# Cross-attention on one core: a reordered and partly rewritten tail for the last four of 64 batches

## The chip, the core and the metric

The kernel runs on one core of a Trainium2 chip. A core has five engines that work beside each other: TensorE (matmuls, PE in the profile, with its weight loads as PEld), VectorE (DVE), ScalarE (ACT), GpSimd (POOL) and SyncE (SP), which here issues all DMAs. Each engine executes its own instructions in the order in which they were written; between engines, semaphores order the work. The metric is device time in microseconds (us), the median of three runs.

## The reference

For each of 64 batches there is a text `x` (256 rows of 512) and a context `c` (256 rows of 384). All is float32.

```python
text_p  = x @ W_text + b_text                      # 256 x 512
audio_p = c @ W_audio + b_audio                    # 256 x 512
Q = layer_norm(text_p, g1, beta1)
K = layer_norm(audio_p, g2, beta2)
alpha = softmax(Q @ K.T / sqrt(512))               # 256 x 256
H = (alpha @ audio_p) @ W_out + b_out
out = layer_norm(H + x, g_out, beta_out)           # 256 x 512
```

Since the rows of `alpha` sum to one, the kernel multiplies `alpha` with `c` itself and folds `W_audio @ W_out` into one weight `wao` and both biases into one row `bao`.

## The kernel before

A batch has two row tiles of 128 rows (`LT = ST = 2`), on 128 partitions. For a batch the kernel computes, in this order:

- the projections q and k, each as seven products of half size (class `Blocks`, `products` on TensorE, L442, `leave` on VectorE, L453, which adds each product into the rows where it belongs). Products 3, 5, 6 and 7 use sums of the input blocks that GpSimd makes beforehand;
- their normalisation on ScalarE and GpSimd. `rstd_of` (L306) is two small GpSimd instructions: L310 or L312 adds the epsilon, L314 raises to the power -0.5;
- a round trip through DRAM in 32 x 32 squares (`store`, `fetch`), and a transpose of the squares on VectorE (`turn`, L91), to get qT and kT; `affine` (L416, ScalarE) applies gamma and beta in four chunks;
- the scores (L481), their row maxima (L491, VectorE), the exponentials with their row sums (L498, ScalarE) and the reciprocals of the sums (L508);
- eT, the transposed exponentials: in the loop by a trip through DRAM, and in the last two batches by TensorE (`transpose_e`, L530) with a copy by ScalarE (`copy_e`, L536);
- the context `ps_z = c.T @ eT` (`context`, L547) and its copy zT (L554, ScalarE);
- the output. In all batches but the last two it is made by the seven products: `start_products` (L556) makes the sums `zsum` (L290 to L293, GpSimd), then `last.o.products` and `last.o.leave`, and `add_x` (L563, GpSimd) adds the input. In the last two batches `multiply(t)` (L593, three matmuls of 512 columns for row tile t) and `evict(t)` (L602, VectorE, which divides by the row sum and adds `x + bao`) do it, and `add_bias` (L655, GpSimd) has made `x + bao` before;
- the last layer norm. For the seven-product batches `statistics` (L565) has ScalarE pass over each row tile twice (L571 for the mean, L576 for the squares); for the last two batches `moments` (L238, L239) takes mean and variance on VectorE. Then VectorE runs `shift` (L618 or L622: minus mean, times gamma) and `settle` (L627: times rstd, plus beta) on each tile; `finish` is both for both tiles;
- `store` (L637), a DMA of the batch's rows.

The order is written out by hand: `tc.manual_schedule()` keeps the instructions of each engine in the order of the program. The loop handles several batches at once (`done` is two batches behind `at`, `last` one behind). It ends with batch 61; the lines from L858 on handle the last four: `done` is batch 60, `last` 61, `at` 62 and `end` 63. The queues that matter there before the change:

- GpSimd: `add_x` of `done`; `add_bias` of 62; rstd of `done`; the four `zsum` of `last`; `add_x` of `last`; `add_bias` of 63; rstd of `last`; rstd of `at`; rstd of each tile of `end`.
- ScalarE: exponentials of `at`; zT of `last`; four passes of statistics of `done`; affine of qT; eT of `at`; affine of kT; zT of `at`; four passes of statistics of `last`; exponentials of `end`.
- SyncE: after the loads of batch 63 only the stores of 60, 61, 62 and of the two tiles of 63.

Buffers are shared in rotation. The output rows (tag `yr`) have two: the tile of `at` reuses that of `done` and waits for its store, and the tile of `end` that of `last`. PSUM has six banks for products, outputs and transposes (`p_pj`) and two for scores and context (`p_at`).

Of the kernel before, what the change touches and what calls it, by code (L numbers as in the profile page):

```python
# [9 lines left out]
F32 = mybir.dt.float32  # L10
AF = mybir.ActivationFunctionType
ALU = mybir.AluOpType
# [3 lines left out]
P = 128  # L16
# [6 lines left out]
def kernel(  # L23
# [41 lines left out]
    nc = tc.nc  # L65
    ctx.enter_context(tc.manual_schedule())
    B, L, D = x.shape
    S, DA = c.shape[1:]
    H = w_text.shape[1]
    LT, ST = L // P, S // P  # L70
    DC, AC, HC = D // P, DA // P, H // P
# [7 lines left out]
    small = ctx.enter_context(tc.tile_pool(name="small", bufs=4))  # L79
    scratch = ctx.enter_context(tc.tile_pool(name="scratch", bufs=3, space=bass.MemoryType.DRAM))  # L80
    p_pj = ctx.enter_context(tc.tile_pool(name="p_pj", bufs=6, space=PSUM))
# [43 lines left out]
    def row(v, name):  # L125
        t = const.tile([P, H], F32, tag=name, name=name)
        nc.sync.dma_start(t, v.rearrange("(o h) -> o h", o=1).broadcast_to([P, H]))
        return t
# [23 lines left out]
    def take_columns():  # L152

        ps = p_at.tile([P, P], F32, tag="at", name="ps_v")
        nc.tensor.transpose(ps, vectors, ident)
        nc.scalar.copy(columns, ps[:, : 5 * HC].rearrange("p (n k) -> p n k", n=5))
        return [columns[:, n, :] for n in range(5)]
# [51 lines left out]
    wao_sb = const.tile([P, AC, D], F32, tag="wao", name="wao")  # L209
# [25 lines left out]
    def moments(mv, src, t):  # L235

        st = small.tile([P, 6], F32, tag="st", name="st")
        nc.vector.bn_stats(st, src)  # L238
        nc.vector.bn_aggr(mv[:, t, :], st)  # L239
# [15 lines left out]
    H2 = H // 2  # L255
# [50 lines left out]
    def rstd_of(var, n, total=False):  # L306

        ve = small.tile([P, n], F32, tag="ve", name="ve")
        if total:
            nc.gpsimd.tensor_scalar(ve, var, 1.0 / D, EPS, ALU.mult, ALU.add)  # L310
        else:
            nc.gpsimd.tensor_scalar(ve, var, EPS, None, ALU.add)  # L312
        r = small.tile([P, n], F32, tag="rstd", name="rstd")
        nc.gpsimd.tensor_tensor(r, ve, nhalf[:, :n], ALU.pow)  # L314
        return [r[:, t : t + 1] for t in range(n)]

    class Projection:
# [40 lines left out]
        def scales(self):  # L358
            if self.centred:
                self.r = rstd_of(self.var, self.nt)  # L360
                return
            self.r = rstd_of(self.mv[:, :, 1], self.nt)
            self.nmr = small.tile([P, self.nt], F32, tag="nmr", name="nmr")
            for t in range(self.nt):
                nc.gpsimd.tensor_scalar(
                    self.nmr[:, t : t + 1],
                    self.mv[:, t, 0:1],
                    self.r[t],
                    -1.0,
                    ALU.mult,  # L370
                    ALU.mult,
                )
# [96 lines left out]
    class Attention:  # L469
# [140 lines left out]
            moments(self.mv, self.y[:, t, :], t)  # L610

        def scales(self, lo=0, n=LT):
            self.r = {lo + t: r for t, r in enumerate(rstd_of(self.mv[:, lo : lo + n, 1], n))}

        def shift(self, t):
            row = self.y[:, t, :]
            if hasattr(self, "o"):
                nc.vector.scalar_tensor_tensor(  # L618
                    row, row, self.nm[:, t : t + 1], go_sb, ALU.add, ALU.mult
                )  # L620
            else:
                nc.vector.scalar_tensor_tensor(  # L622
                    row, row, self.mv[:, t, 0:1], go_sb, ALU.subtract, ALU.mult
                )
# [27 lines left out]
    def add_bias(b):  # L652
        xb = rows[b][0]
        for t in range(LT):
            nc.gpsimd.tensor_tensor(xb[:, t, :], xb[:, t, :], bao_sb, ALU.add)  # L655

    assert B > 3
    q, k, xT, cT, rows = {}, {}, {}, {}, {0: (x_0, c_0)}
# [61 lines left out]
    g1_sb, be1_sb, g2_sb, be2_sb, bac_sb = take_columns()  # L720
# [45 lines left out]
    beo_sb = row(beta_out, "beo")  # L766

    done = last = None
    for b in range(B - 2):
        three = b + 3 < B  # L770
        at = Attention(b)
# [83 lines left out]
        done, last = last, at  # L855


    at = Attention(B - 2)  # L858
# [8 lines left out]
    last.turn_e()  # L867
    at.maxima()
    at.exponentials()
    add_bias(B - 2)  # L870
    last.context()
    done.statistics()
    at.reciprocals()
    q[B - 1].turn()
    last.start_products()
    q[B - 1].affine(g1_sb, be1_sb)
    at.transpose_e()
    at.copy_e()
    last.o.products(1, 2)
    last.o.leave(1)  # L880
    last.o.products(6, 5)
    k[B - 1].turn()
    last.o.leave(6)
    last.o.leave(2)
    last.o.leave(5)
    last.o.products(7, 3)
    last.o.leave(3)
    last.o.leave(7)
    last.o.products(4)
    last.o.leave(4)  # L890
    last.add_x()
    k[B - 1].affine(g2_sb, be2_sb)
    add_bias(B - 1)
    at.context()
    done.finish()
    done.store()
    end = Attention(B - 1)
    end.scores(end=True)
    at.start_output()
    at.multiply(0)  # L900
    last.statistics()
    end.maxima()
    end.exponentials()
    end.reciprocals()
    at.evict(0)
    at.multiply(1)
    end.transpose_e()
    end.copy_e()
    last.finish()
    last.store()  # L910
    at.evict(1)
    at.scales()
    end.context()
    at.finish()
    at.store()
    end.start_output()
    for t in range(LT):
        end.multiply(t)
        end.evict(t)
        end.scales(t, 1)  # L920
        end.finish(t, 1)
        end.store(t, 1)


# [30 lines left out]
```

## Time and profile before

| what | value |
|---|---|
| time, median of 3 runs | 1429.02 us (1428.93 to 1429.34) |
| the profiled execution, its time | 1430.98 us |
| its span in the profile | 1429.2 us |
| busy over the span: PE, DVE, ACT, POOL | 98%, 89%, 66%, 61% |
| scores of batch 62 end | 1384.4 us |
| scores of batch 63 end | 1405.3 us |
| last matmul ends | 1419.67 us |
| last VectorE instruction ends | 1426.16 us |

In the profile a line such as `L627 DVE` is an instruction of that line of the kernel before on that engine. Times in the chain and the timeline are microseconds from the start of the span. The chain is followed back from the last instruction: at each step to what released it, or to the instruction before it on its engine. A TensorE matmul in float32 is recorded as two instructions, so 128 x 256 columns twice is one matmul of the program.

### The profile page before, as it was taken

How to read it: one execution, taken by the hardware profiler on the slowest of the kernel's cores; microseconds unless marked ns; L12 is line 12 of the kernel's file. 1: busy time of each engine (PE TensorE's matmuls, PEld its weight loads, DVE VectorE, ACT ScalarE, POOL GpSimd, SP SyncE). 2: the span in 40 equal slices, each digit the busy share in tenths (PEclk: the TensorE clock that was granted, in tenths of full speed). 3: DMA queues.
4: the chain of work that ended last, by engine and by line, in shares of the span. 5: the costliest groups of instructions: out<-in, count | busy, mean ns of one | idle time of the engine just before them, and what ended most of it. 6: DMA issues, size and time to landing. Idle time of an engine off the chain costs nothing.

```text
span 1429.2 us, 23268 instructions
## 1 busy us (share of the span) xinstructions
PE 1406.8 (98%) x6419; PEld 1219.1 (85%) x6419; DVE 1270.3 (89%) x2123; ACT 937.5 (66%) x2309; POOL 874.7 (61%) x1293
## 2 busy tenths in 40 slices
PE   7999999999999999999999999999999999999997
PEld 4788888888888888888888888888888888888874
DVE  5789999999999999999999999999999999999976
ACT  4576676676676676676676766766766766766762
POOL 4556666666666666666666566576566566666643
PEclk9999999999999999999999999999999999999998
DMA  9798787887887788788788788888878888877761
GB/s 206 215 250 232 232 239 221 234 242 218 238 234 229 231 230 235 231 231 235 227 224 243 232 223 242 236 221 240 240 223 232 246 219 232 242 221 231 222 191 60
DMA packets 450294, 322.61 MB, mean 226 GB/s; under 512 B 154740, under 2 KB 382580, under 8 KB 450164
## 3 DMA queue, kind: packets, MB, share of 16 engines
q1 hardware_dynamic: 450164, 321.11, 79.8%
q8 instruction: 53, 0.87, 0.3%
q14 instruction: 77, 0.63, 0.2%
HBM read 204.09 MB, written 116.92 MB: 225 GB/s over the span
## 4 chain that ended last, share of the span: by engine, by line
PE 96%; DVE 1%; DMA 1%; POOL 0%; ACT 0%; SPq 0%; issue 0%; POOLq 0%; DVEq 0%
PE ps_q L442 27%; PE ps_k L442 21%; PE ps_y L442 21%; PE ps_sc L481 15%; PE ps_z L547 11%; DMA wt<-in_L_xattn_W_text_dram 1%; PE ps_wao L216 1%; PE ps_q L332 0%; DVE yr L627 0%; DVE yr L618 0%; DVE y L602 0%; DVE st L238 0%; DMA out_dram<-yr 0%; DVE y L627 0%; POOL ve L312 0%
## 5 line engine op out<-in xcount | busy, mean ns | idle before, releaser
L481 PE MATMUL ps_sc<-kT,qT 128*128 128x256 f32 x1024 | 231.7, 379 | 0.0
L312 POOL TENSOR_SCALAR ve<-var 128x2 f32<-128x2 f32 x126 | 44.9, 356 | 304.1 <-ACT junk L350 304.1
L498 ACT ACTIVATE e<-ps_sc,nmx 128x256 f32<-128x256 f32 x128 | 59.5, 469 | 247.5 <-DVE nmx L491 247.5
L453 DVE TENSOR_TENSOR qr<-ps_q,qr 128x512 f32<-128x512 f32 x378 | 188.2, 511 | 35.8 <-PE ps_q L442 23.8
L481 PEld LDWEIGHTS ps_sc<-kT,qT 128*128 128x128 f32 x1024 | 194.2, 190 | 27.6 <-ACT kT L416 0.9
L453 DVE TENSOR_TENSOR kr<-ps_k,kr 128x512 f32<-128x512 f32 x378 | 188.1, 511 | 24.3 <-PE ps_k L442 0.5
L453 DVE TENSOR_TENSOR yr<-ps_y,yr 128x512 f32<-128x512 f32 x372 | 185.1, 511 | 27.5 <-PE ps_y L442 3.8
L563 POOL TENSOR_TENSOR yr<-yr,x 128x512 f32<-128x512 f32 x124 | 156.9, 1275 | 62.9 <-DVE yr L453 62.9
L547 PE MATMUL ps_z<-eT,c 128*128 128x256 f32 x768 | 176.6, 379 | 0.8 <-ACT eT L536 0.7
L442 PE MATMUL ps_q<-wtsum,xsum 128*128 128x256 f32 x756 | 173.4, 379 | 0.0
L314 POOL TENSOR_TENSOR rstd<-ve,nhalf 128x2 f32<-128x2 f32 (+1 forms) x193 | 158.6, 822 | 16.1
L442 PE MATMUL ps_k<-wa,cT 128*128 128x256 f32 x630 | 166.8, 379 | 0.0
L442 PE MATMUL ps_y<-wao,zT 128*128 128x256 f32 x620 | 164.7, 380 | 0.0
L547 PEld LDWEIGHTS ps_z<-eT,c 128*128 128x128 f32 x768 | 145.8, 190 | 21.2 <-ACT eT L536 0.9
L442 PEld LDWEIGHTS ps_q<-wtsum,xsum 128*128 128x128 f32 x756 | 143.6, 190 | 19.5
L350 ACT ACTIVATE junk<-kr 128x512 f32<-128x512 f32 x126 | 79.4, 630 | 98.0 <-DVE kr L453 98.0
L442 PEld LDWEIGHTS ps_k<-wa,cT 128*128 128x128 f32 x630 | 119.6, 190 | 16.2
L416 ACT ACTIVATE qT<-qT,columns 128x256 f32<-128x256 f32 x256 | 133.0, 592 | 0.4 <-DVE qT L91 0.4
L378 ACT ACTIVATE kr<-kr,rstd 128x512 f32<-128x512 f32 x126 | 84.0, 714 | 74.8 <-POOL rstd L314 74.8
L416 ACT ACTIVATE kT<-kT,columns 128x256 f32<-128x256 f32 x256 | 132.3, 590 | 0.4 <-DVE kT L91 0.3
L442 PEld LDWEIGHTS ps_y<-wao,zT 128*128 128x128 f32 x620 | 118.2, 191 | 16.2
L627 DVE SCALAR_TENSOR_TENSOR yr<-yr,rstd,beo 128x512 f32<-128x512 f32 x124 | 128.3, 1071 | 0.3
(140 smaller groups left out, 2944.8 us busy)
## 6 DMA issues: line engine op xcount, KB each, us to landing
x<-in_x_dram SPq DMA_DIRECT2D x64, 512.0 KB, 4.3
kd<-kr SPq DMA_DIRECT2D x64, 512.0 KB, 3.1
kq<-kd SPq DMA_DIRECT2D x256, 128.0 KB, 3.4
qd<-qr SPq DMA_DIRECT2D x64, 512.0 KB, 5.1
qq<-qd SPq DMA_DIRECT2D x256, 128.0 KB, 3.3
xq<-in_x_dram SPq DMA_DIRECT2D x252, 128.0 KB, 2.8
out_dram<-yr SPq DMA_DIRECT2D x62, 512.0 KB, 4.8
cq<-in_ctx_dram SPq DMA_DIRECT2D x252, 96.0 KB, 2.5
```

Of the source, the lines that this page charges most:

```text
L312: nc.gpsimd.tensor_scalar(ve, var, EPS, None, ALU.add)
L314: nc.gpsimd.tensor_tensor(r, ve, nhalf[:, :n], ALU.pow)
L350: nc.scalar.activation(junk, self.rows[:, t, :], AF.Square, scale=1.0 / math.sqrt(H), accum_out=self.var[:, t : t + 1],)
L378: nc.scalar.mul(row, row, self.r[t])
L416: nc.scalar.activation(self.T[:, k, :], self.T[:, k, :], AF.Identity, bias=bet[:, k : k + 1], scale=gam[:, k : k + 1],)
L442: nc.tensor.matmul(bank[:, j, :], lhsT=side, rhs=w, start=(i == 0), stop=(i == len(pairs) - 1))
L453: add = lambda o, i0, i1: nc.vector.tensor_tensor(o, i0, i1, ALU.add)
L481: nc.tensor.matmul(self.sc[:, t, :], lhsT=self.qT[:, k, bass.ts(t, P)], rhs=self.kT[:, k, :], start=(k == 0), stop=(k == HC - 1),)
L498: nc.scalar.activation(self.e[:, t, :], self.sc[:, t, :], AF.Exp, bias=self.nmx[:, t : t + 1], accum_out=self.den[:, t : t + 1],)
L547: nc.tensor.matmul(ps[:, j, :], lhsT=self.c_sb[:, s, bass.ts(lo + j, P)], rhs=self.eT[:, s, :], start=(s == 0), stop=(s == ST - 1),)
L563: nc.gpsimd.tensor_tensor(self.y[:, t, :], self.y[:, t, :], self.xb[:, t, :], ALU.add)
L627: nc.vector.scalar_tensor_tensor(self.y[:, t, :], self.y[:, t, :], self.r[t], beo_sb, ALU.mult, ALU.add)
```

## The change

Nothing in the loop changes but a test of an attribute (`shift` picks its mean from `nm`, which `statistics` sets, or else from `mv`). In the tail:

- `done` and `last` take their statistics by `moments` on VectorE instead of `statistics` on ScalarE. The new method also issues their rstd at once. For `done` this comes ahead of `reciprocals` of `at` and, on GpSimd, ahead of `add_bias(B - 2)`; for `last` it comes behind `exponentials` of `end`.
- `done.finish()` is taken apart: both shifts stand ahead of `start_products`, both settles where `finish` stood.
- Product 4 of `last` is multiplied as the third, ahead of 6 and 5. The transposes of q and k (`turn`) and their `affine` move: q behind the first products, k behind `leave(2)`.
- `end.transpose_e` and `end.copy_e` come between `at.multiply(0)` and `at.multiply(1)`.
- The start and the first product of `end`'s output stand ahead of `at.finish()`.
- The second tile of `end` is multiplied, evicted, settled and stored in two halves of 256 columns; its statistics are two `bn_stats` joined by one `bn_aggr`. The work on the two tiles of `end` is interleaved.

```diff
         def scales(self, lo=0, n=LT):
-            self.r = {lo + t: r for t, r in enumerate(rstd_of(self.mv[:, lo : lo + n, 1], n))}
+            self.r = getattr(self, "r", {})
+            self.r.update({lo + t: r for t, r in enumerate(rstd_of(self.mv[:, lo : lo + n, 1], n))})
+
+        def moments(self):
+            self.mv = small.tile([P, LT, 2], F32, tag="mvy", name="mvy")
+            for t in range(LT):
+                moments(self.mv, self.y[:, t, :], t)
+            self.scales()
+
+        def multiply_halves(self, t):
+            self.ps_h = []
+            for h in range(2):
+                ps = p_pj.tile([P, H2], F32, tag="pj", name="ps_y")
+                self.ps_h.append(ps)
+                for k in range(AC):
+                    nc.tensor.matmul(
+                        ps,
+                        lhsT=self.zT[:, k, bass.ts(t, P)],
+                        rhs=wao_sb[:, k, bass.ts(h, H2)],
+                        start=(k == 0),
+                        stop=(k == AC - 1),
+                    )
+
+        def evict_halves(self, t):
+            st = small.tile([P, 2, 6], F32, tag="st2", name="st2")
+            for h in range(2):
+                half = self.y[:, t, bass.ts(h, H2)]
+                nc.vector.scalar_tensor_tensor(
+                    half,
+                    self.ps_h[h],
+                    self.rden[:, t : t + 1],
+                    self.xb[:, t, bass.ts(h, H2)],
+                    ALU.mult,
+                    ALU.add,
+                )
+                nc.vector.bn_stats(st[:, h, :], half)
+            nc.vector.bn_aggr(self.mv[:, t, :], st)
+
+        def settle_halves(self, t):
+            for h in range(2):
+                half = self.y[:, t, bass.ts(h, H2)]
+                nc.vector.scalar_tensor_tensor(
+                    half, half, self.r[t], beo_sb[:, bass.ts(h, H2)], ALU.mult, ALU.add
+                )
+                nc.sync.dma_start(out[self.b, bass.ts(t, P), bass.ts(h, H2)], half)
...
     at.exponentials()
+    done.moments()
+    at.reciprocals()
     add_bias(B - 2)
     last.context()
-    done.statistics()
-    at.reciprocals()
-    q[B - 1].turn()
+    done.shift(0)
+    done.shift(1)
     last.start_products()
-    q[B - 1].affine(g1_sb, be1_sb)
     at.transpose_e()
     at.copy_e()
     last.o.products(1, 2)
+    q[B - 1].turn()
     last.o.leave(1)
+    last.o.products(4)
+    q[B - 1].affine(g1_sb, be1_sb)
     last.o.products(6, 5)
-    k[B - 1].turn()
     last.o.leave(6)
     last.o.leave(2)
+    k[B - 1].turn()
+    k[B - 1].affine(g2_sb, be2_sb)
     last.o.leave(5)
     last.o.products(7, 3)
     last.o.leave(3)
     last.o.leave(7)
-    last.o.products(4)
     last.o.leave(4)
     last.add_x()
-    k[B - 1].affine(g2_sb, be2_sb)
     add_bias(B - 1)
     at.context()
-    done.finish()
+    done.settle(0)
+    done.settle(1)
     done.store()
     end = Attention(B - 1)
     end.scores(end=True)
     at.start_output()
     at.multiply(0)
-    last.statistics()
     end.maxima()
     end.exponentials()
+    last.moments()
     end.reciprocals()
     at.evict(0)
-    at.multiply(1)
     end.transpose_e()
     end.copy_e()
+    at.multiply(1)
     last.finish()
     last.store()
     at.evict(1)
     at.scales()
     end.context()
+    end.start_output()
+    end.multiply(0)
     at.finish()
     at.store()
-    end.start_output()
-    for t in range(LT):
-        end.multiply(t)
-        end.evict(t)
-        end.scales(t, 1)
-        end.finish(t, 1)
-        end.store(t, 1)
+    end.evict(0)
+    end.scales(0, 1)
+    end.multiply_halves(1)
+    end.shift(0)
+    end.evict_halves(1)
+    end.scales(1, 1)
+    end.settle(0)
+    end.store(0, 1)
+    end.shift(1)
+    end.settle_halves(1)
```

More of the change, by code (lines that the diff above doesn't have):

```diff
@@ L612, in scales @@
         def scales(self, lo=0, n=LT):
-            self.r = {lo + t: r for t, r in enumerate(rstd_of(self.mv[:, lo : lo + n, 1], n))}
+            self.r = getattr(self, "r", {})
[39 more added lines that the diff above has]
+                nc.sync.dma_start(out[self.b, bass.ts(t, P), bass.ts(h, H2)], half)
         def shift(self, t):
             row = self.y[:, t, :]
-            if hasattr(self, "o"):
+            if hasattr(self, "nm"):
                 nc.vector.scalar_tensor_tensor(
```

## The prediction

> **What bounds the kernel now.** I read the page first, then the chain of waits and the timeline of the last 50 us, then the windows there. The page says that TensorE is the bound for the whole (busy 98% of the span, 96% of the chain). The change leaves everything up to the scores of batch 62 as it was, so only what follows 1384.4 us of the 1429.2 us span can move. Batches 60, 61, 62, 63 are `done`, `last`, `at`, `end` there. The chain in order of time, where it leaves TensorE:
>
> ```profile
> 1387.82 1.23 ACT junk L571 x4
> 1389.05 1.42 ACT junk L576 x4
> 1390.46 0.08 issue
> 1390.54 0.20 POOL ve L310
> 1390.74 0.07 issue
> 1390.82 0.70 POOL rstd L314
> 1391.52 0.43 POOL zsum L290
> 1391.94 0.07 issue
> 1392.01 0.47 POOL zsum L291
> 1392.48 0.04 issue
> 1392.52 6.77 PE ps_y L442 x16
> ```
>
> ScalarE's statistics of `done` hold the rstd in POOL's queue, and `zsum` stands behind it, so TensorE has nothing from 1389.14 to 1392.52, 3.38 us. The windows over that stretch show what follows; the columns are length, busy time and count of the five engines, the granted TensorE clock, DMA share and GB/s:
>
> ```profile
> 1389.00:1392.50 3.50, 0.14 (x1) 0.00 (x0) 1.79 (x3) 3.50 (x10) 1.80 (x5) 0.91 0.84 271
> 1392.50:1395.00 2.50, 2.48 (x6) 2.03 (x7) 0.69 (x1) 2.16 (x5) 1.07 (x2) 0.50 0.03 11
> ```
>
> The clock falls to half. Windows of half a microsecond put the fall at 1391.87 and the return at 1398.69, 6.82 us later, twice 3.41. So 16 matmul records took 6.77 us where 16 at full clock take 16 x 0.2155 = 3.45 (0.2155 is the start-to-start distance of 128x256 records in the scores).
>
> The timeline shows two more costs, POOL beside VectorE, and a store:
>
> ```profile
> 1384.39 2.49 POOL L655 TENSOR_TENSOR x<-x,bao 128x512 f32<-128x512 f32 x2
> ...
> 1400.50 1.57 DVE L627 SCALAR_TENSOR_TENSOR yr<-yr,rstd,beo 128x512 f32<-128x512 f32 x1
> ...
> 1401.49 3.41 POOL L655 TENSOR_TENSOR x<-x,bao 128x512 f32<-128x512 f32 x2
> ...
> 1408.34 0.75 DVE L602 SCALAR_TENSOR_TENSOR y<-ps_y,rden,x 128x512 f32<-128x512 f32 x1 [1.04 <-DMA out_dram<-yr]
> ```
>
> Alone, `add_bias` takes 2.49 and an L627 0.75; together 3.41 and 1.57. The store of `done` (issued 1405.47, 2.75 to land) holds the first output tile of `at` until 1408.34. From there to the end VectorE is the chain: 9.90 us to the first L602 of `end` at 1418.24, 7.92 for the two tiles of `end` to 1426.16, 3.04 for the last store and the end of the program.
>
> **The change, part by part.** All times stand on the profiled execution's axis.
>
> *Statistics of `done` to VectorE.* Two pairs at the row of L238/L239 (0.694 and 0.182, 0.92 a pair with gaps) follow the maximum of `at`, which ends at 1385.17: they end at 1386.93. They had no cover before and need none: VectorE idled there (2.0 us before the qT transpose, which waits for its DMA until 1388.41). Two shifts come next, to 1388.45, and just fit. ScalarE is free of 2.65 us: the copy of eT runs at 1387.9 instead of 1392.33.
>
> *What this does to POOL's queue.* The rstd of `done` is now **ahead of `add_bias`** of batch 62, which before filled 1384.39 to 1386.89 while ScalarE worked. Behind the waiting L312 stand `add_bias` and `zsum`, and TensorE waits for `zsum`. L312: 0.22 alone, 0.62 to 0.78 with a two-input VectorE operation running (a shift starts just then); L314 0.70 alone, 1.15 beside shifts; `add_bias` 2.5. So `zsum` starts between 1390.5 and 1391.5; 0.99 more for its first two sums. TensorE's product 6 starts between 1391.5 and 1392.5. I take 1392.15, nearer the upper end, since the shifts do run beside it. That is only **0.4 us earlier than before**: the sums are not "at once".
>
> *Product 4 moved ahead.* It needs no `zsum`. Its two matmuls (4 records, 0.86 us) now run before the gap, which shrinks from 3.38 to 2.15 us (1390.0 to 1392.15), and leaves 12 records behind it instead of 16.
>
> *The clock.* Here the row and a rule part. In the 3.41 us window ending at 1391.87 TensorE was busy 0.69 us, 20%, and the clock fell; in the prologue a window of 66% busy passed. The changed kernel puts 1.55 us there, 45%. By interpolation between these rows it is a toss-up. The Trainium skill (TensorE: Matmul & The Clock Gate, "Why this matters for your kernels") says that gaps up to about 3 us keep the full clock, that is, no fall with a gap of 2.15. By the rule the end is 1423.4; by the 20% row, two slow windows, 1426.2. I lean to the rule, since 45% is already over the middle of 20 and 66.
>
> *From 1392.15 at full clock.* TensorE: 6 matmuls of products, 6 of the context, 8 of the scores, 20 x 0.431 = 8.62, and 0.17 to drain: scores of `end` at 1400.94, before 1405.32. VectorE: L453 of product 6 at 1393.66 (its bank is released after product 5); the kT transpose, now queued behind products 6 and 2, 1394.73 to 1395.97 (before 1391.95); four affines to 1398.05, just behind which the scores pass (they start at 1397.32 and wait for kT chunk by chunk, so it costs at most 0.1). The remaining four L453 end at 1397.95, then two settles beside POOL's `add_x` and `add_bias`, 1.6 each as above, to 1401.2. I price them contended; the skill (SBUF — State Buffer, "Who interferes with whom") would have one side fully blocked, 1.27 + 0.75 = 2.0 each, 0.8 worse in sum; the trace has 1.57 to 1.76, and that decides. Store lands at 1401.25 + 2.75 = 1404.0. The two pairs for `last` (1.84) plus maximum and reciprocal end at 1403.76, under that landing. First L602 of `at`: 1404.1, **4.2 earlier**.
>
> *Transposes between the output tiles.* ps_e moves ahead of the second product, so eT's copy and the gap of 0.7 us at 1410.90 vanish. It buys nothing alone: VectorE's 9.90 us to the tiles of `end` are the same instructions, and TensorE is done with them long before.
>
> *Last tile in halves.* VectorE before: 7.92 us, of which two waits for rstd of 0.77 and 0.78. Now: L602, two bn operations and a shift of tile 0 take 2.4; two half evictions and two half bn (0.48 and 0.43 each: full rows minus 256 columns, 0.267, by the L453 pair 0.691 and 0.424) and an aggregate to 4.4; settle 0 and shift 1 to 5.8; the rstd of tile 1 by 6.0; two halves of 0.48 to 6.85. **1.1 less**. The last store carries half the bytes: 2.75 instead of 3.04 as an estimate from 256 KB moving in about 0.7 us. Three stores instead of two at 0.35 of SP each lie apart.
>
> Sum: 4.2 + 1.1 + 0.3 = **5.6**, so a span of 1423.6. The profiled execution took 1430.98, 1.78 around its span and 1.96 above the median 1429.02. I assume both offsets stay: 1423.4.
>
> **Rivals.**
>
> *The clock falls all the same, two windows* (to 1398.69). Products 6 and 5 end at 1395.0, 7 and 3 at 1397.3; the context runs half cold to 1400.56, the scores to 1404.17; first L602 at 1406.9, 1.4 earlier; with the end 2.8 in all: 1426.2. For it: the 20% row. If 1391.87 to 1395.28 counts as busy enough, one window: L602 at 1405.35, 1424.7. Against that: an 81% busy window did not bring the clock back before.
>
> *A new wait for the old.* POOL's queue (rstd, then `add_bias` beside shifts) puts the sums at 1391.6, the clock falls twice, the halves gain nothing: L602 about 1407.3, 1428.0, within 0.2%.
>
> *Slower.* The clock, once down at 1391.87, stays there. Each further window of 3.41 us in which TensorE bounds costs 1.71. From 1426.2 it takes more than three of them (5.7 us) to lie 0.2% over the time before; four give 1433.0. For it: 81% did not suffice. Against: the first full window did, and the changed order leaves no gap after 1392.15.
>
> **How the numbers follow.** Under 0.2% (2.9 us) this kernel can't be told from no change: its runs spread over 0.4 us, and the offset of a profile is 2. Full clock 0.55 (own range 1422 to 1424.5, from the start of product 6 at 1391.5 to 1392.5 and contended or free settles); one slow window 0.13; two 0.19, lying on the limit 1426.2, half of it counted faster; nothing gained 0.09; slower 0.04. Faster: 0.54 + 0.12 + 0.09 + 0.01 = 0.76; same 0.20. The range takes the full clock's lower end with free settles, 1421.8, to two windows with a late product 6, 1427.0.
>
> **What would show it.** Right: POOL's L312 right behind VectorE's second aggregate near 1387, then both `add_bias`, `zsum` near 1391; a TensorE gap near 2.2 us; clock 1.00 from 1392 to 1399; first L602 of `at` near 1404, released by the store. Wrong: a clock of 0.50 after the gap; `zsum` before 1390 or after 1392; scores waiting for kT's affine by over 0.3; the end of `end` over 7.3 us long; a settle of 0.75.

## The result, and the profile after

| | before | after |
|---|---|---|
| time, median of 15 runs | 1429.34 us (1427.46 to 1430.74) | 1425.55 us (1424.08 to 1428.58) |
| ratio after to before | | 0.9975, 95% interval 0.9968 to 0.9981 |
| profiled execution, its time and span | 1430.98, 1429.2 us | 1424.23, 1422.3 us |
| end of the scores of batch 62 (E62) | 1384.44 | 1383.40 |
| from E62 to the end of the span ("the tail") | 44.76 us | 38.92 us |

The change makes the kernel 3.8 us faster (2.7 to 4.6 by the interval); the range held it, the likeliest time, 1423.4, was 2.1 too low. In the two profiled executions the tails differ by 5.84 us, so the two traces show more of a gain than the medians do. That is the question for the experiments.

Line numbers of the kernel after lie higher: L602 stays, L618/L622 is L666, L627 is L671, L655 is L699. The chain of waits of the kernel after, in order of time (start, length, what):

```profile
1385.82 0.69 POOL ve L312
1386.52 0.07 issue
1386.59 1.07 POOL rstd L314
1387.66 2.46 POOL x L699 x2
1390.12 0.42 POOL zsum L290
1390.55 0.07 issue
1390.61 0.46 POOL zsum L291
1391.08 0.04 issue
1391.12 2.86 PE ps_y L442 x12
1393.98 2.59 PE ps_z L547 x12
1396.57 3.45 PE ps_sc L481 x16
1400.02 2.59 PE ps_y L593 x6
1402.61 0.03 issue
1402.63 0.76 DVE y L602
```

ScalarE's four passes are gone from it. In their place stand the rstd, slow beside the shifts, and both `add_bias`. Counted from E62 (here and below), the first `zsum` starts at 6.68 instead of 7.04: 0.36 earlier. Then TensorE runs without a break, 12 records in 2.86 us. The window of 3.41 us that holds most of the gap, with the granted clock after the five engines:

```profile
1389.66:1393.07 3.41, 1.95 (x9) 1.75 (x10) 0.35 (x1) 0.72 (x2) 2.42 (x5) 1.00 0.39 142
```

The clock stays at 1.00. The timeline of VectorE at the settles of batch 60, and the first output tile of batch 62:

```profile
1396.96 2.47 DVE L671 SCALAR_TENSOR_TENSOR yr<-yr,rstd,beo 128x512 f32<-128x512 f32 x2
...
1402.63 0.75 DVE L602 SCALAR_TENSOR_TENSOR y<-ps_y,rden,x 128x512 f32<-128x512 f32 x1 [0.22 <-PE ps_y L593]
```

The two settles take 2.47 from start to end, one 0.80 and one 1.75. The store was issued at 1399.46 and no longer releases L602; the product does.

### The profile page after: what moved, and what is told of

Same layout as the page of the kernel before. It is cut to its first block, busy times and chain, and to the rows that moved or that the text cites. A ratio compares the mean times of both kernels' runs of the same rounds, so it can differ in the third digit from the quotient of the medians.

```text
span 1422.3 us, 23273 instructions
## 1 busy us (share of the span) xinstructions
PE 1402.4 (99%) x6425; PEld 1217.7 (86%) x6425; DVE 1271.6 (89%) x2134; ACT 932.5 (66%) x2293; POOL 873.2 (61%) x1293
## 4 chain that ended last, share of the span: by engine, by line
PE 97%; DVE 1%; DMA 1%; POOL 0%; SPq 0%; issue 0%; POOLq 0%; ACT 0%; DVEq 0%
PE ps_q L442 27%; PE ps_k L442 21%; PE ps_y L442 21%; PE ps_sc L481 16%; PE ps_z L547 11%; PE ps_wao L216 1%; DMA wt<-in_L_xattn_W_text_dram 1%; PE ps_q L332 0%; DVE st L238 0%; DMA cq<-in_ctx_dram 0%; PE ps_y L593 0%; POOL x L699 0%; DVE y L602 0%; POOL ve L312 0%; POOL rstd L314 0%
## 5 line engine op out<-in xcount | busy, mean ns | idle before, releaser
L671 DVE SCALAR_TENSOR_TENSOR yr<-yr,rstd,beo 128x512 f32<-128x512 f32 x124 | 127.1, 1063 | 0.1
```

What stands on the lines that cost most here:

```text
L671: nc.vector.scalar_tensor_tensor(self.y[:, t, :], self.y[:, t, :], self.r[t], beo_sb, ALU.mult, ALU.add)
```

## The experiments

All kernels but three were timed in several rounds against the kernel before on the same chip; the last three have one time and a trace. The names: b_ builds on the kernel before, a_ on the changed one, s_ on a_sums. The place of each step in the tail, from one trace each, in us after E62:

| kernel | TensorE gap | clock at 0.50 | scores of 63 end | first L602 of 62 | first L602 of 63 | last VectorE instruction ends | tail |
|---|---|---|---|---|---|---|---|
| before | 3.38 | 6.83 | 20.88 | 23.91 | 33.80 | 41.72 | 44.76 |
| before_2 | 3.39 | 3.41 | 19.54 | 22.85 | 32.75 | 40.68 | 43.71 |
| b_fill | 0.79 | none | 17.85 | 21.56 | 31.46 | 39.38 | 42.41 |
| b_p4 | 2.52 | none | 16.99 | 21.53 | 31.43 | 39.36 | 42.39 |
| after, after_2, after_3 | 2.15, 2.16, 2.16 | none | 16.62 | 19.24 | 29.14 | 36.19 | 38.92 to 38.94 |
| a_p4_late | 3.02 | 6.83 | 20.40 | 23.01 | 32.91 | 39.96 | 42.70 |
| a_act | 2.52 | 3.41 | 18.48 | 23.99 | 33.89 | 40.94 | 43.67 |
| a_sums | none | none | 14.20 | 16.81 | 26.72 | 33.77 | 36.50 |
| s_pse_old | none | none | 14.20 | 16.82 | 26.72 | 33.77 | 36.52 |
| s_whole | none | none | 14.20 | 16.81 | 26.72 | 33.32 | 36.35 |
| s_fin | none | none | 14.20 | 16.81 | 26.29 | 33.34 | 36.07 |
| best | none | none | 14.20 | 16.81 | 26.29 | 32.89 | 35.92 |

The gap is the idle time of TensorE ahead of product 6. The clock column has the us at half clock between this gap and the end of TensorE's work. All these stretches are 3.41 us long or twice that; below, 3.41 us at half clock are called a slow window.

**b_fill: TensorE kept busy in the gap.**

```diff
     last.o.products(1, 2)
+    filler = p_pj.tile([P, H2], F32, tag="pj", name="ps_fill")
+    for i in range(6):
+        nc.tensor.matmul(
+            filler, lhsT=last.zT[:, 0, :P], rhs=wao_sb[:, 0, :H2], start=True, stop=True
+        )
     last.o.leave(1)
```

> The kernel before, with six idle matmuls of 128x256 (2.6 us) put on TensorE behind products 1 and 2 of batch 61, into a bank that nobody reads; all else is as before. Theory A (the clock): the sums come when they came, but TensorE's gap of 3.4 us shrinks to about 0.8, so the clock stays at 1.00 and the products behind it take 3.4 us instead of 6.8: 3 us less than an execution with two slow windows, and in the median 1.5 to 3 less than 1429.3, about 1427; the single times lie closer together. Theory B (the clock costs nothing that counts, only the time of the sums does): 1429.3, within 0.5.

Measured: 1428.87 against 1429.85 before, ratio 0.9992 (0.9983 to 1.0001). The sums came at 7.04 as before, the clock stayed at 1.00, and the scores of 63 ended 3.03 us earlier than in the first trace: the stage behaves as theory A says. But the first L602 came only 2.35 earlier, and the median says 1.0, not clear of nothing. The median alone does not exclude theory B. The mean granted clock, which is on record for every run, helps: of the 27 runs of the kernel before on this chip, seven have 0.998, which leaves no room for a slow window (the sum is at after_2), with a median of 1428.66, like b_fill; six have 0.995, as the first trace with its two slow windows, and a median of 1430.84. So the clock costs some 2 us at the end, in the executions in which it falls, and less there than where it strikes.

**b_p4: product 4 early, alone.**

```diff
     last.o.products(1, 2)
     last.o.leave(1)
+    last.o.products(4)
     last.o.products(6, 5)
...
     last.o.leave(7)
-    last.o.products(4)
     last.o.leave(4)
```

> The kernel before with product 4 of batch 61 multiplied ahead of 6 and 5, and nothing else. Theory A: the gap is 2.5 us instead of 3.4, 0.86 us of work leaves the path and the clock falls in fewer executions: 1.5 to 2 less than 1429.3, about 1427.6. Theory B: 0.9 less, 1428.4.

Measured: 1429.33, ratio 1.0000 (0.9991 to 1.0009). The gain of theory A lies outside the interval, that of theory B, 0.9 us, just inside, but nothing of it is seen. The trace tells why. The scores of 63 end 0.86 earlier than those of b_fill, one product, and its first L602 comes at the same place. The chain of waits of b_p4:

```profile
1395.33 0.81 DVE yr L618
1396.14 0.03 issue
...
1396.23 1.58 DVE yr L627
1397.81 1.69 DVE yr L618
1399.53 1.65 DVE yr L627
1401.19 2.75 DMA out_dram<-yr
1403.94 0.03 issue
1403.97 0.05 DVEq L602
1404.02 0.04 issue
1404.06 0.76 DVE y L602
```

With the clock up, VectorE sets the time: the four shifts and settles of batch 60, three of them at 1.6 to 1.8 us beside GpSimd, and then the store of 60. The chain of the kernel before runs through the same shifts, settles and store, but behind TensorE's slow products. With these at full clock, VectorE's queue is a second bound, which holds the first L602 at 21.5 us after E62 in b_fill and in b_p4 alike. All that TensorE wins ahead of it in that kernel stops there.

**a_p4_late: product 4 late again in the changed kernel.**

```diff
     last.o.leave(1)
-    last.o.products(4)
...
     last.o.leave(7)
+    last.o.products(4)
     last.o.leave(4)
```

> The changed kernel with product 4 back in its old place, last. Theory A: the gap is 3.0 us instead of 2.15 and the clock falls in most executions: 0.9 for the product and 1 to 2 for the clock, about 1427.3 against 1425.5. Theory B: 0.9 more, 1426.4.

Measured: 1427.85 against 1429.85, ratio 0.9986 (0.9978 to 0.9995); the changed kernel has 0.9975, so 0.0011 or 1.6 us lie between them, between A's 1.8 and B's 0.9 and not telling them apart. The trace does: `zsum` at 6.69 as in the changed kernel, a gap of 3.02, and the clock at half for two windows:

```profile
1387.83:1391.25 3.42, 1.31 (x7) 0.80 (x5) 2.12 (x3) 2.06 (x4) 3.42 (x4) 1.00 1.03 262
1391.25:1394.66 3.41, 2.50 (x6) 2.04 (x7) 0.00 (x0) 0.60 (x2) 1.87 (x4) 0.50 0.28 104
1394.66:1398.07 3.41, 3.41 (x9) 2.65 (x9) 2.81 (x5) 0.61 (x2) 0.00 (x0) 0.50 0.00 0
```

In this execution it cost 3.77 us at the first L602, and all of it reached the end (42.70 against 38.92): the changed kernel has no second bound close behind. That is one execution with two slow windows. By the mean granted clock (at after_2) seven of the 11 runs of a_p4_late had a slow window or two (0.996 or 0.997) and four none (0.998), with medians of 1427.97 and 1426.28. So the clock falls in most executions, as theory A has it. A step that buys nothing measurable in the kernel before (b_p4) is worth 1.6 us by the medians in the changed one, and 3.8 where it keeps the clock from falling for two windows.

**a_act: the statistics of batch 60 back on ScalarE.** `finish` takes shifts and settles together again.

```diff
-    done.moments()
     at.reciprocals()
...
     last.context()
-    done.shift(0)
-    done.shift(1)
+    done.statistics()
...
-    done.settle(0)
-    done.settle(1)
+    done.finish()
```

> The changed kernel with the statistics of batch 60 back on ScalarE, where they stood, and shifts and settles of 60 together behind the seven products, as before the change; product 4 stays early, batch 61 keeps its statistics on VectorE. Theory A (what moving the statistics buys is not the sums but that the two shifts run early, away from GpSimd): product 6 only 0.4 us later, but four two-input operations beside GpSimd instead of two, 1.6 us each; the store of 60 and with it the first L602 of batch 62 come 3.5 to 4 us later: 22.6 to 23.1 us behind the end of the scores of 62 instead of 19.2; about 1429. Theory B (it buys the sums alone): 0.4 to 0.8 more than the changed kernel, 1426.2.

Measured: 1428.48 against 1430.64 on its chip, ratio 0.9990 (0.9981 to 0.9998), so 2.1 us over the changed kernel by the two ratios. In the trace the first L602 comes at 23.99, 4.75 later, of which 1.36 is one slow window (products 6 and 5 took 2.94 us instead of 1.58, their time in b_p4 at full clock) and 0.37 the later start of product 6 (8.09 instead of 7.72). The rest, 3.0, is VectorE and the store, in the timeline of VectorE:

```profile
1399.48 0.80 DVE L662 SCALAR_TENSOR_TENSOR yr<-yr,nm,go 128x512 f32<-128x512 f32 x1
1400.39 1.57 DVE L671 SCALAR_TENSOR_TENSOR yr<-yr,rstd,beo 128x512 f32<-128x512 f32 x1
1401.88 1.75 DVE L662 SCALAR_TENSOR_TENSOR yr<-yr,nm,go 128x512 f32<-128x512 f32 x1
1403.66 1.64 DVE L671 SCALAR_TENSOR_TENSOR yr<-yr,rstd,beo 128x512 f32<-128x512 f32 x1
...
1408.18 0.75 DVE L602 SCALAR_TENSOR_TENSOR y<-ps_y,rden,x 128x512 f32<-128x512 f32 x1 [0.62 <-DMA out_dram<-yr]
```

Theory A: what the moved statistics buy is mostly that the shifts run early, in time that VectorE had idle, and only for a small part the 0.36 us of the sums. The 3.0 is from one trace; the ratios carry 2.1 in all, and their intervals, which meet at 0.9981, anything from nothing to 4.3.

**a_sums: the sums wait for nothing but zT.** `moments` no longer calls `scales`, which is called apart.

```diff
+    add_bias(B - 2)
     done.moments()
     at.reciprocals()
-    add_bias(B - 2)
...
     last.start_products()
+    done.scales()
...
     last.moments()
+    last.scales()
```

> The changed kernel with the two additions x + bao of batch 62 on GpSimd ahead of the rstd of batch 60, as before the change, and both rstds (of 60 and 61) issued apart: that of 60 behind the four sums. The sums then wait for nothing but zT. Theory A: no gap on TensorE over 0.5 us, product 6 about 2 us earlier, first L602 of batch 62 about 2 us earlier, clock 1.00 in every execution: about 1422.5, and single times within 2 us. Theory B (VectorE's queue bounds the tail, so earlier sums buy nothing): 1425.5, within 0.5.

Measured: 1423.07 (1422.58 to 1424.11) against 1429.85, ratio 0.9956 (0.9944 to 0.9969). `zsum` starts at 2.43 instead of 6.68, TensorE has no gap, and everything from the first L602 on lies 2.42 earlier than in the changed kernel. Theory A. The chain of waits there is TensorE without a break:

```profile
1387.59 4.75 PE ps_y L442 x22
1392.34 2.59 PE ps_z L547 x12
1394.93 3.45 PE ps_sc L481 x16
1398.39 2.59 PE ps_y L593 x6
```

**s_whole: the last tile whole, the interleaving kept.** On a_sums:

```diff
-    end.multiply_halves(1)
+    end.multiply(1)
     end.shift(0)
-    end.evict_halves(1)
+    end.evict(1)
...
-    end.settle_halves(1)
+    end.settle(1)
+    end.store(1, 1)
```

> The kernel with the sums first (a_sums), but the second tile of batch 63 whole again: multiplied, evicted, settled and stored as one tile of 512 columns, still interleaved with the first tile. It has no gap on TensorE, so the clock plays no part. Theory H (the halves shorten the end): 1.0 us or more over a_sums, 1424.2, and over 8 us from the first L602 of batch 63 to the end of VectorE. Theory I (the interleaving does it, the halves add two instructions and their fixed cost for what the half store saves): within 0.3 of a_sums, 1423.1; from the first L602 of 63 to VectorE's end 6.65 instead of 7.05, and 0.3 more from there to the end.

Measured: 1421.97 against 1430.64, ratio 0.9950 (0.9938 to 0.9963); the tail is 0.15 shorter than that of a_sums. From the first L602 of 63 to the end of VectorE it takes 6.60 us with the tile whole and 7.05 with halves; from there to the end of the span 3.03 and 2.73. The halves lose 0.45 and win 0.30. Theory I: this stretch is 1.3 us shorter than in the kernel before (7.92) with the interleaving alone, which fills the waits for rstd with work of the other tile; the halves take 0.45 of that back.

**s_pse_old: the transposes behind the second product again.** On a_sums, `end.transpose_e()` and `end.copy_e()` change places with `at.multiply(1)`.

> The kernel with the sums first, but the transposes of batch 63 behind the second product of batch 62 again. Theory: TensorE gets back a gap of 0.7 us while it waits for the copy of eT, and ends 0.7 us later, but VectorE's chain hides it: within 0.2 of a_sums, 1423.1. Rival (TensorE's end counts): 0.7 more, 1423.8.

Measured: 1423.72 against 1430.64, ratio 0.9956 (0.9943 to 0.9970), like a_sums. TensorE gets its gap of 0.68 back and ends 0.94 later (28.64 instead of 27.70 after E62), and no VectorE instruction from the first L602 of 63 on moves by as much as 0.01. This part of the change is hidden.

**s_fin: both shifts of batch 62 ahead of its settles.** On a_sums:

```diff
-    at.finish()
+    at.shift(0)
+    at.shift(1)
+    at.settle(0)
+    at.settle(1)
```

> The kernel with the sums first, and for batch 62 both shifts ahead of both settles, so that the wait of the first settle for its rstd (0.9 us on VectorE) is filled by the second shift. Theory: VectorE's chain sets the end there: 0.7 less than a_sums, 1422.4, and from the second L602 of 62 to the first L602 of 63 4.6 us instead of 5.35. Rival (TensorE or a store is what the end waits for): 1423.1.

Measured: 1422.46 against 1430.64, ratio 0.9950 (0.9938 to 0.9963). In the trace the first L602 of 63 comes 0.43 earlier, and so does the end: the theory's place, at 0.43 instead of 0.7. The median alone, with its interval, would not tell it from a_sums.

**best: a_sums, s_whole and s_fin together.**

> All that the runs so far speak for: the sums first, both shifts of batch 62 ahead of its settles, the second tile of batch 63 whole. Theory (these are three separate stretches of one chain): 36.5 us from the end of the scores of 62 to the end, less 0.43 for the shifts and 0.15 for the whole tile, 35.9; about 1422.0, clock 1.00 until TensorE is done. Rival (they hide each other): 36.1 to 36.4, 1422.5.

Measured: 1422.21 (1421.63 to 1423.10) against 1430.23, ratio 0.9943 (0.9930 to 0.9957), and a tail of 35.92, which is 36.50 - 0.43 - 0.15. The parts add. It lies ahead of the kernel before by 8 us; the changed kernel has 0.9975 (0.9968 to 0.9981), measured apart from it, and the intervals don't meet.

**after_2, after_3, before_2: the same two kernels again, for their traces.**

> The changed kernel once more, unchanged, for a second trace. Theory (the clock looks at fixed windows of 3.41 us, whose place against the gap differs from execution to execution; it falls behind a window in which TensorE was busy 0.38 or less, holds at 0.53 or more): the gap is again 2.15 us and lies wholly in one window about every second time; then the clock is 0.50 for one window and the tail 40.2 to 40.6 us long, otherwise 38.9 as in the first trace. Rival (a gap of 2.15 never lets the clock fall): 38.9 in each trace.

> The same for a third trace: as for the second, by the place of its windows.

> The kernel before once more, for a second trace. Theory: the gap of 3.38 us lets the clock fall in almost every execution, for one window or two by the place of the windows; with two the tail is 44.8 us as in the first trace, with one 43.2 to 43.7. Rival (it is always two): 44.8.

Measured: 1426.39 and 1427.23 for the changed kernel, 1429.53 for the one before. In before_2 the clock fell for one window, and the tail is 43.71, as its theory has it. In after_2 and after_3 it did not fall: three traces of three are on the rival's side. But after_2 was near a fall. Its window in which the gap lies, and that of before_2:

```profile
1389.63:1393.04 3.41, 1.41 (x7) 0.90 (x5) 1.38 (x2) 2.08 (x4) 3.33 (x5) 1.00 0.97 278
1393.04:1396.45 3.41, 3.25 (x15) 2.89 (x16) 1.61 (x3) 0.00 (x0) 1.20 (x3) 1.00 0.11 40
```

```profile
1389.83:1393.24 3.41, 1.11 (x5) 1.01 (x6) 1.25 (x1) 3.41 (x9) 2.87 (x6) 1.00 0.55 201
1393.24:1396.66 3.42, 3.42 (x10) 2.71 (x9) 1.51 (x4) 1.23 (x3) 0.00 (x0) 0.50 0.00 0
```

1.41 of 3.41 us, 41%, held; 1.11, 33%, did not (the other traces have 20, 36 and 38% before a fall, 53% and more without). A gap of 2.16 that lies wholly in one window leaves 37%, and no trace of the changed kernel had that. The timed runs tell whether others did, by the mean granted clock over the span that is on record for each. In the traces of the changed kernel and of the gapless ones this mean is 0.998 or 0.999; the clock falls only when TensorE is done. One slow window takes off another 0.0012 (half of 3.41 us in 1422). The kernel before has 0.995 in its trace with two slow windows and 0.996 in that with one; without any it has 0.9974 to 0.9986, with one 0.9962 to 0.9974. This is an estimate from its trace: 9.5 us lie between the last matmul and the end of the span, and by the shares above the clock falls 2.0 to 5.5 us into them.

| mean granted clock of the run | kernel after, 15 runs | kernels without a gap (a_sums, s_, best), 25 runs | kernel before, 51 runs on three chips |
|---|---|---|---|
| 0.998 or 0.999 | 10, median 1425.10 us | 25 | 13, median 1428.66 us |
| 0.996 or 0.997 | 5, median 1426.27 us | none | 26, median 1430.09 us |
| 0.995 or less | none | none | 12, median 1430.95 us |

The five runs of the changed kernel with 0.997 are the five slowest of its 15. No trace shows a fall anywhere but behind the gap and at the end. So the clock does fall in about a third of its executions, for one window, and the theory holds (it said half); the three traces are of the other two thirds. The kernel before kept its clock in about a quarter of its runs. With three digits on record, the counts may be off by a run or two at the borders.

The three tails are equal to 0.02 us, while the three times are 1424.23, 1426.39 and 1427.23. All of that difference lies before E62: 1383.40, 1385.47 and 1386.31.

## Why the prediction was right or wrong

**Direction, most of the path and the length of the tail: right.** Counted from E62, the prediction had VectorE's second aggregate at 2.49 (measured 2.34), product 6 at 7.71 (7.72), a gap of 2.15 (2.15), the scores of 63 at 16.50 (16.62), kT's affine at 13.6 (13.74), the first L602 at 19.7 (19.24), 9.90 us from there to batch 63 (9.90), and a tail of 39.2 (38.92). That the sums would come only 0.4 us earlier, because the rstd now stands ahead of `add_bias` in GpSimd's queue, is what the chain shows, and a_sums shows what that order costs: 2.4 us.

**Wrong: "I assume both offsets stay".** This step carried the gain of one trace, 5.6 us, to the median. The trace before was one with two slow windows; before_2 had one and a tail 1.05 shorter, and about a quarter of its runs had none, which leaves a tail of 42.4 if b_fill and b_p4 are taken for it. Against these three the changed kernel's 38.93 gains 5.8, 4.8 and 3.5 us. The time before was thus not the time of that trace, and the time after is not that of the three traces either, since a third of the runs has a slow window. The medians, 3.8 apart (2.7 to 4.6), compare two such mixtures; the runs with no slow window on either side, of separate sets, are 3.6 apart. That the start became slower is a rival which the traces suggest (E62 at 1383.6 in the mean of the four of the kernels b_ and before, 1384.9 in the ten others). The runs do not bear it out: span less tail puts E62 at 1384.1 in the ten runs of the changed kernel with no slow window, at 1384.6 in the 13 such runs of the kernel before and in the 25 of the gapless kernels.

**Wrong: "its runs spread over 0.4 us".** Three runs showed that; 15 runs spread over 3.3 before and 4.5 after. Part is the clock, as the table shows. The traces place the rest: from the maxima of batch 10 to those of batch 62 before, after, after_2, after_3 and before_2 take 1120.94 to 1120.95 us, all the same; the maxima of batch 2 already begin between 89.1 and 93.9, those of batch 10 between 262.5 and 265.4. So it arises in the first 265 us, most of it in the first 94; what causes it is open.

**Right by luck: "The clock".** The forecast of 1.00 held in all three traces of the changed kernel, and by the mean clock failed in five of 15 runs. The reason given was the rule of the Trainium skill (TensorE: Matmul & The Clock Gate, "Why this matters for your kernels") that gaps up to about 3 us keep the clock. The rule is not sharp enough: a gap of 2.52 us kept it in b_p4 (the two windows it touched were busy 73% and 53%) and lost it in a_act (36%), and 2.15 us lost it in those five runs. What decides in these traces is the share in one window of 3.41 us, and where the windows lie differs from execution to execution. The prediction took their place from one trace: it had 45% in the window of the gap, where the three traces have 57, 41 and 53%.

**Half wrong: "Last tile in halves ... 1.1 less".** The stretch was 0.87 shorter on VectorE (7.05, forecast 6.85) and 0.30 in the store, as forecast; but the credit belongs to the interleaving. With the tile whole the two are 6.60 and 3.03, 0.15 less in sum.

**Wrong by a little:** two settles "beside POOL's `add_x` and `add_bias`, 1.6 each" were 0.80 and 1.75; so the store was early enough, and the product, not the store, released L602 (0.4 us). The timeline shows why, with the two settles and between them the second half of `add_x`:

```profile
1396.96 0.80 DVE L671 SCALAR_TENSOR_TENSOR yr<-yr,rstd,beo 128x512 f32<-128x512 f32 x1
1397.17 1.71 POOL L563 TENSOR_TENSOR yr<-yr,x 128x512 f32<-128x512 f32 x1
1397.69 1.75 DVE L671 SCALAR_TENSOR_TENSOR yr<-yr,rstd,beo 128x512 f32<-128x512 f32 x1
```

Alone an `add_x` takes 1.27 and a settle 0.75. The one here ends 1.12 us behind the end of the first settle, and the second settle 0.55 behind the end of that `add_x`: each got going only when the other engine was all but done. These two figures give the ends of all six such instructions of the kernel before from 1399.8 to 1405.4 within 0.02 us. So the trace agrees with the skill's rule (SBUF — State Buffer, "Who interferes with whom") that VectorE with two inputs in SBUF and a GpSimd instruction that reads SBUF share a port pair under an exclusive lock. The prediction read it as 2.0 each and set it aside; what is lost is only what is left of the other's instruction, less some 0.2: 0.05 us for the first settle, which met the last 0.25 us of an `add_x`, and 1.0 for the second. Its 1.57, too, is a settle beside `add_x`, not beside `add_bias`.

**The rivals.** Two slow windows were not seen in the changed kernel; a_p4_late shows what they would look like. One slow window, which had 0.13, came in a third of the runs. "Transposes ... buys nothing" is shown by s_pse_old. That the clock stays down was not seen: in all four traces in which it fell, a window busy 90% or more brought it back.

**Priced only in part:** VectorE's `finish` of batch 60 and its store. The prediction had the store in its chain, but not that VectorE's queue holds the first L602 of the kernel before at 21.5 us after E62 even at full clock. That hides part of what the clock costs there (3.03 us at the scores, 2.35 at the first L602). For the same reason the early shifts, which the prediction gave no time of their own, are worth 3.0 us in the trace of a_act.

## What to carry to other kernels

Before pricing a wait, ask what stands second behind it: remove it alone (b_fill, b_p4), and the next bound may keep the time. An instruction that moves to another engine changes the queues on both sides; here the two small rstd operations, moved ahead of additions that nobody waited for, held four sums, a matmul gap and 2.4 us. Where a program has gaps and a long start, compare stretches of traces from a common point, and don't carry the difference of two single traces to the medians: the mean granted clock of each timed run tells which kind of execution a trace has caught.

## What the hardware showed that was not expected

- The TensorE clock changed on a grid of 3.41 us windows in these traces: the slow stretches are 3.41 and 6.83 us. Around the gap it fell behind windows in which TensorE was busy 20 (before), 33 (before_2), 36 (a_act) and 38% (a_p4_late), and held behind 41 (after_2), 53 (after_3, b_p4) and 57% (after). It stayed down behind windows that were busy 73 (a_p4_late) and 81% (before), and came back behind 90 (a_act) and 100%. So it takes more to bring it back than to keep it, and the limit for falling lies between 38 and 41% in these traces. The same gap of 2.15 us costs nothing or a slow window, by where it lies in the grid.
- Half a tile is far from half the time on VectorE: the eviction of 512 columns (L602) takes 0.745 us, of 256 0.479 and 0.467; bn_stats 0.694 and 0.428.
- VectorE and GpSimd take turns where both read two float32 tiles: in the kernels before and after, the later one ended 0.55 us (settle or shift) or 1.12 us (`add_x`, `add_bias`) behind the end of the other. Small instructions wait as well: the power of the rstd on GpSimd takes 0.70 us alone and 1.07 behind a shift, its epsilon 0.22 and 0.69, while the shift, which came first, keeps its 0.73 to 0.74.
